# One edge tile in 44 fetched row by row from ScalarE's queue, and PSUM copies moved from ScalarE to VectorE

## The chip, the cores and the metric

The kernel runs on one core of one Trainium2 chip. The metric is the time of one execution in device microseconds (us). A core has these engines, each with its own instruction queue: TensorE (PE; its weight loads are listed as PEld), VectorE (DVE), ScalarE (ACT), GpSimd (POOL) and SyncE (SP). SP, ACT and POOL can start DMA transfers, which 16 DMA engines carry out. Engines wait for each other through semaphores.

## The reference

One layer of a relational graph network with a pre-normalization, on 12500 nodes of 256 features and 212500 edges of 8 types. Edges are sorted by destination; each node has one edge to itself as the last of its edges.

```python
h = jnp.maximum(_layernorm(x, axis=-1), 0.0)
hx = jnp.einsum('ni,rio->rno', h, weight)            # 8 relations
msg = hx[edge_type, src]
agg = jax.ops.segment_sum(msg, dst, num_segments=num_nodes)
node_repr = agg * 0.5 ** 0.5 + h_bias + (h @ loop_weight) * 0.5 ** 0.5
return x + node_repr
```

All arithmetic of the features is in float32.

## The kernel before

The order is turned round: rows of `h` are first summed by destination and type, and the sums are then multiplied by the weights.

**Edge tiles.** The edges are cut into 792 units, and each unit into two tiles (`PAIR`) of up to 128 edges, 1583 tiles in all. 128 units form a block; for each block the positions, sources and types of its edges are worked out on VectorE ahead of time (`prepare`), by small steps in a list named `background`. The sources end as a table `gidx[b]`, turned so that one column holds the 128 sources of a tile. Tile t stands in block t // 256.

**Fetching.** `gather(t)` (L779) issues one indirect DMA from POOL (L791): 128 rows of 1 KB, by the column of `gidx`, into the buffer `msg[t]`. There are buffers for 66 tiles, and the gather of tile t + 64 is issued in the turn of tile t, so it waits until PE has done with the buffer's former tiles. The first 100 tiles fetch rows of `x` and normalize them (L753); all later ones fetch rows of `h32`, the normalized table in DRAM that the kernel writes at its beginning.

**Sums by destination.** For each tile, VectorE makes one-hot rows (`onehots`, L804, four tiles at once), and PE multiplies the fetched rows with them (`edge_sums`, L837). The two tiles of a unit add up in one PSUM bank `ps`, four of which take turns. VectorE then adds the bank into a ring of sums in SBUF at an offset read from a register (`add_sums`, L851); 16 offsets at a time are loaded into VectorE's registers (L816).

**Products.** The nodes form 98 groups of 128. When a group's sums are complete, PE multiplies them with the weights of the 8 types and of the loop (L1029, 36 matmul instructions a group, spread over the following tiles by a budget), and VectorE adds the result to `x` (L1041, L1042). Six groups have their place in the ring.

**Starting a group.** `begin(g)` turns the group's rows of `h` on PE (`turn_nodes`, L878, into the PSUM bank `pt`). VectorE writes the rows, masked by the type of each node's own edge, into the ring as first values (`own`, L900, eight instructions), and ACT copies them to `self_t` (`keep`, L883), from which the loop product is made. The types come from `find_types`, once for four groups: a small product on PE (L934), some VectorE instructions (`kinds_of`), four ACT instructions that write a diagonal matrix (L954), a product that spreads it (L961) and an ACT copy `types` (L965). All these use the one bank `pt`; `shared` puts such jobs one behind the other, each with a first step and later steps some tiles afterwards.

**Order.** The whole program is unrolled, and its order written out by hand: one turn of the loop `for t in range(NT)` (L1186) per edge tile, in which every engine's queue gets its next instructions. ACT also issues 34 small transfers named `spans` (L353) for later blocks; SP issues all other plain transfers, among them three of a single row (L346).

Of the kernel before, what the change touches and what calls it, by code (L numbers as in the profile page):

```python
# [8 lines left out]

F32 = mybir.dt.float32  # L10
BF16 = mybir.dt.bfloat16
I32 = mybir.dt.int32
AF = mybir.ActivationFunctionType
ALU = mybir.AluOpType
# [2 lines left out]
DRAM = bass.MemoryType.DRAM  # L17
SYNC_DEP = mybir.DependencyInfo(mybir.DependencyClass.Sync, mybir.DependencyReason.DATA)
DVE = mybir.EngineType.DVE

P = 128
EPS = 1e-5
# [3 lines left out]
XG = 4  # L26
# [20 lines left out]

MSGS = 66
AHEAD = 64

QUAD = 4
LEAD = 4
# [167 lines left out]
def kernel(  # L220
# [32 lines left out]
    dram = ctx.enter_context(tc.tile_pool(name="dram", bufs=1, space=DRAM))  # L253

    h32 = dram.tile([N, D], F32, name="h32")

    const = ctx.enter_context(tc.tile_pool(name="const", bufs=1))
    ident = const.tile([P, P], F32, name="ident")
# [25 lines left out]
    with ExitStack() as main:  # L284
# [29 lines left out]
        msg, oh, offsets, kind = {}, {}, {}, {}  # L314
        firsts, stops, loops, marked, typed, gidx, col = {}, {}, {}, {}, {}, {}, {}
        added, zeroed = {}, {}
        state = {"h32": None}


# [52 lines left out]
        def core(got, name):  # L372

            return got[name][:, BEFORE : BEFORE + EDGES]

        def compacted(got, bit, bits, n):

# [9 lines left out]
        def sources(b, got):  # L387


            if b == 0:  # L390
                def copy():
                    nc.vector.tensor_copy(work_tile(got, "sf", 2)[:, :U], got["s"][:, :U])

                return [copy, *turned(
                    got, "sf", lambda: gidx.setdefault(b, idx.tile([P, U], I32, name="gidx")))]

            def rises():
                nc.vector.tensor_tensor(
                    work_tile(got, "rise", 0), got["d"][:, 1:], got["d"][:, :WIDE], op=ALU.subtract)

            def spans():
                got["from_"] = small.tile([P, 1], F32, name="from_")
                nc.vector.tensor_tensor(got["from_"], got["spans"][:, 0:1], steps, op=ALU.add)
                got["kept"] = small.tile([P, 1], F32, name="kept")
                nc.vector.tensor_tensor(
                    got["kept"], got["spans"][:, 0:1], got["spans"][:, 1:2], op=ALU.subtract)
                nc.vector.tensor_scalar(
                    got["kept"], got["kept"], most, limit if b == NB - 1 else float(U),
                    op0=ALU.add, op1=ALU.min)

            def stays():
                nc.vector.tensor_scalar(
                    work_tile(got, "stay", 1), got["rise"], 0.0, None, op0=ALU.is_equal)
                firsts[b] = small.tile([P, 1], F32, name="firsts")
                nc.vector.tensor_copy(firsts[b], got["d"][:, BEFORE : BEFORE + 1])

            def shifts():
                nc.vector.scalar_tensor_tensor(
                    work_tile(got, "code", 2), got["d"][:, :WIDE], got["from_"], got["stay"],
                    op0=ALU.subtract, op1=ALU.mult)  # L420

            def codes():
                nc.vector.scalar_tensor_tensor(
                    got["code"], got["code"], float(R), got["t"][:, :WIDE], op0=ALU.mult, op1=ALU.add)

            def packs():
                nc.vector.scalar_tensor_tensor(
                    packed, got["s"][:, :WIDE], float(1 << (TB + SB)), got["code"],
                    op0=ALU.mult, op1=ALU.add)

            def unpacks():
                nc.vector.tensor_single_scalar(
                    work_tile(got, "from", 5, I32)[:, :U], packed[:, :U], TB + SB,
                    op=ALU.logical_shift_right)
                nc.vector.tensor_scalar(
                    work_tile(got, "sf", 2)[:, :U], got["from"][:, :U], 0.0, float(N - 1),
                    op0=ALU.max, op1=ALU.min)
                nc.vector.tensor_single_scalar(
                    work_tile(got, "rest", 3, I32)[:, :U], packed[:, :U], (1 << (TB + SB)) - 1,
                    op=ALU.bitwise_and)  # L440

            return [rises, spans, stays, shifts, codes, packs, *compacted(got, TB, SB, WIDE), unpacks,
                    *turned(got, "sf", lambda: gidx.setdefault(b, idx.tile([P, U], I32, name="gidx")))]

        def last_edges(b, got):

# [332 lines left out]
        def gather(t):  # L779
            if t % PAIR == 0:  # L780
                both = msgs.tile([P, PAIR, D], F32, name="msg")
                for i in range(PAIR):
                    msg[t + i] = both[:, i, :]
            if t % QUAD:
                kind[t] = kind[t - 1]
            else:
                kind[t] = "h" if state["h32"] is not None and t >= state["h32"] + LATE else "x"
            table = {"h": h32, "x": x}[kind[t]]
            b, i, u = place_of(t)
            at = i * P + u  # L790
            nc.gpsimd.indirect_dma_start(  # L791
                out=msg[t], out_offset=None, in_=table[:, :],
                in_offset=bass.IndirectOffsetOnAxis(ap=gidx[b][:, at : at + 1], axis=0))

        def onehots(t):

# [25 lines left out]
        def edge_sums(t):  # L822
            m, o = msg.pop(t), oh.pop(t)
            if t % PAIR == 0:
                bank = banks[t // PAIR % BANKS]
                sums["ps"] = bank[:, : KC * R * WIN].rearrange("p (c k) -> p c k", c=KC)
            ps = sums["ps"]
            i = t % PAIR
            width = R * (REACH[0][1] if i and t // (PAIR * P) < NB - 1 else WIN)
            end = t == NT - 1 or i == PAIR - 1  # L830
            free = added.get(t // PAIR - BANKS)
            if i == 0 and free is not None and latest["pe"] is not None:
                tc.add_manual_dep(latest["pe"], free.name, SYNC_DEP, reason="bank is free")
            if i == 0 and latest["pe"] is not None:
                tc.add_manual_dep(latest["pe"], made[t], SYNC_DEP, reason="one-hots are made")
            for c in range(KC):
                j = nc.tensor.matmul(  # L837
                    ps[:, c, :width], m[:, c * P : (c + 1) * P], o[:, :width],
                    start=(i == 0 and c == 0), stop=(end and c == KC - 1))
            latest["pe"] = j.ins  # L840
            return ps

        sums = {}
# [23 lines left out]
            i = nc.scalar.activation(a, zero.unsqueeze(2).to_broadcast([P, KC * R, GROUP]), AF.Copy)  # L867
            zeroed[g, "slot"] = i.ins

        def turn_nodes(g, pool, written=None):  # L870

            n = plan.ends[g] - plan.starts[g]
            pst = pt[:, : KC * P].rearrange("p (c d) -> p c d", c=KC)

            def turn():
                rows_ = got["h", g // XG][:, g % XG, :]
                for c in range(KC):
                    nc.tensor.transpose(  # L878
                        pst[:, c, :n], rows_[:n, c * P : (c + 1) * P], ident[:n, :n])

            def keep():
                got["self", g] = pool.tile([P, KC, GROUP], F32, name="self_t")
                i = nc.scalar.activation(got["self", g][:, :, :n], pst[:, :, :n], AF.Copy)  # L883
                if written:
                    tc.add_manual_dep(
                        i.ins, written[0].name, SYNC_DEP, reason="one reader at a time")

            return turn, keep, pst

        def begin(g):  # L890

            n = plan.ends[g] - plan.starts[g]
            q, k = divmod(g, XG)
            written = []
            turn, keep, pst = turn_nodes(g, selves, written)
            s0 = g % SLOTS * GROUP

            def own(r):
# [3 lines left out]
                    op0=ALU.is_equal, op1=ALU.mult)  # L902
                if r == R - 1:
                    zeroed[g, "slot"] = i.ins
                    written.append(i.ins)

            def write():
                for r in range(R):
# [17 lines left out]
        def find_types(q):  # L926
# [11 lines left out]
            def kinds_of():  # L938
# [11 lines left out]
                nc.vector.tensor_reduce(kinds, one, AX.X, ALU.add)  # L950
                marked[q] = marks.tile(
                    [P, 2, XG * GROUP], BF16, tag="mark0", name="diagonal")[:, 0, :]
                for g in range(XG):
                    nc.scalar.activation(  # L954
                        marked[q][:, g * GROUP : (g + 1) * GROUP], ident, AF.Copy,
                        scale=kinds[:, g : g + 1])

            shared(find, [(2, kinds_of)])

# [2 lines left out]

            def types_of():
                typed[q] = types.tile([P, XG * GROUP], BF16, name="types")
                nc.scalar.activation(typed[q], pt, AF.Copy)  # L965

            shared(spread, [(1, types_of)], lambda: q in marked, wait=2 * SETTLE)

        got = {}

# [14 lines left out]
        def group_ahead(g):  # L985
# [11 lines left out]
            if q < plan.typed:  # L997
                def turned_nodes():
                    turn, keep, _ = turn_nodes(g, early)
                    shared(turn, [(1, keep)])  # L1000

                work.append((0.4, turned_nodes))
            if k == XG - 2:
# [70 lines left out]
        with tc.manual_schedule():  # L1074
# [111 lines left out]
            for t in range(NT):  # L1186
                done["tile"] = t
                if t + AHEAD < NT:
                    gather(t + AHEAD)
                blocks_ahead(t)  # L1190
                credit = min(0.0, credit) + SHARE - (0.52 if t % PAIR else 0.0)
                for f in after:
# [110 lines left out]
```

## Time and profile before

| | us |
|---|---|
| median of 3 runs (2438.91 to 2439.70) | 2439.66 |
| the profiled execution | 2440.51 |
| its span, first to last instruction | 2438.7 |
| PE busy, matmuls (10339 instructions) | 1934.7 |
| VectorE busy (3382) | 1326.8 |
| ACT busy (475) | 222.2 |
| POOL busy (1609) | 1508.5 |

The mean clock granted to TensorE is 0.893 of full speed. Busy times are of the engines' own work; instructions that only wait, branch, load registers or issue a DMA are not in them, with one exception: POOL's indirect DMAs are counted. A row of a group names the line, the engine, the operation, what it writes and reads, its count, its busy time and mean duration in ns, and the idle time of the engine before it with what ended most of that. "Issue" stands for idle time in which the engine waited for nothing that the profile shows, and "remote" for a release that the profile can't assign. The times of PE are those at which its instructions start; their ends are modelled.

### The profile page before, as it was taken

How to read it: one execution, taken by the hardware profiler on the slowest of the kernel's cores; microseconds unless marked ns; L12 is line 12 of the kernel's file. 1: busy time of each engine (PE TensorE's matmuls, PEld its weight loads, DVE VectorE, ACT ScalarE, POOL GpSimd, SP SyncE). 2: the span in 40 equal slices, each digit the busy share in tenths (PEclk: the TensorE clock that was granted, in tenths of full speed). 3: DMA queues.
4: the chain of work that ended last, by engine and by line, in shares of the span. 5: the costliest groups of instructions: out<-in, count | busy, mean ns of one | idle time of the engine just before them, and what ended most of it. 6: DMA issues, size and time to landing. Idle time of an engine off the chain costs nothing.

```text
span 2438.7 us, 28985 instructions
## 1 busy us (share of the span) xinstructions
PE 1934.7 (79%) x10339; PEld 1700.9 (70%) x10339; DVE 1326.8 (54%) x3382; ACT 222.2 (9%) x475; POOL 1508.5 (62%) x1609
## 2 busy tenths in 40 slices
PE   0257788787888888888888888888888888888889
PEld 0246677776777777777777777777777777777788
DVE  3387734546744545754445754445754445765453
ACT  3474310000000000000000000000000000000000
POOL 7535666666666666666666666666666666666640
PEclk9557989999989898998889998899899889998999
DMA  6584433343334343333343333343333343333320
GB/s 204 161 296 137 125 89 117 89 127 114 91 117 119 89 124 116 91 117 105 105 123 91 116 116 93 115 127 89 117 117 89 118 118 92 117 106 101 111 71 14
DMA packets 147869, 278.87 MB, mean 114 GB/s; under 512 B 29759, under 2 KB 97064, under 8 KB 147720
## 3 DMA queue, kind: packets, MB, share of 16 engines
q0 software_dynamic: 75984, 207.59, 29.2%
q1 hardware_dynamic: 70136, 69.38, 8.9%
q8 instruction: 82, 1.34, 0.2%
q14 instruction: 67, 0.55, 0.1%
q10 hardware_dynamic: 1600, 0.01, 0.0%
HBM read 251.26 MB, written 25.60 MB: 114 GB/s over the span
## 4 chain that ended last, share of the span: by engine, by line
PE 66%; issue 14%; DVE 11%; another core or an unknown queue 4%; ACT 2%; DMA 1%; POOL 1%; DVEq 0%; SPq 0%; ACTq 0%; POOLq 0%
PE ps L837 33%; PE po L1029 31%; DVE acc L851 2%; DVE oh L804 1%; DVE e_stats L741 1%; DVE acc L900 1%; PE pt L878 1%; DVE n_stats L741 1%; DVE moves L380 1%; DVE n_mv L743 1%; POOL msg L791 1%; DMA w<-in_L_gnn_weight_dram 1%; DVE fixed L382 0%; ACT diagonal L954 0%
## 5 line engine op out<-in xcount | busy, mean ns | idle before, releaser
L791 POOL DMA_INDIRECT msg<-h,gidx x1483 | 1411.6, 952 | 761.5 <-issue 389.6
L837 PE MATMUL ps<-oh,msg 128*128 128x176 f32 (+1 forms) x6332 | 1178.9, 314 | 303.2 <-issue 163.0
L837 PEld LDWEIGHTS ps<-oh,msg 128*128 128x128 f32 x6332 | 1090.1, 208 | 444.6 <-issue 217.5
L1029 PE MATMUL po<-w,acc 128*128 128x256 f32 x3136 | 975.0, 413 | 87.5 <-issue 75.5
L851 DVE TENSOR_TENSOR acc<-acc,ps 128x352 f32 x792 | 409.0, 516 | 764.4 <-remote 377.3
L1029 PEld LDWEIGHTS po<-w,acc 128*128 128x128 f32 x3136 | 577.8, 206 | 164.8 <-issue 132.2
L804 DVE TENSOR_TENSOR oh<-fixed,cols 128x704 f32<-128x704 f32 x397 | 348.9, 879 | 0.0
L900 DVE SCALAR_TENSOR_TENSOR acc<-types,pt 128x256 f32<-128x256 bf16 (+1 forms) x688 | 248.7, 411 | 89.2 <-PE ps L837 48.5
L883 ACT ACTIVATE self_t<-pt 128x256 f32<-128x256 f32 x98 | 37.5, 383 | 1754.2 <-DVE acc L900 1030.5
L791 POOL DMA_INDIRECT msg<-in_x_dram,gidx x100 | 95.0, 950 | 83.1 <-issue 49.3
L1029 PE MATMUL po<-wl,self_t 128*128 128x256 f32 x392 | 116.6, 410 | 14.3 <-issue 7.7
L1029 PEld LDWEIGHTS po<-wl,self_t 128*128 128x128 f32 x392 | 70.9, 201 | 35.5 <-issue 24.0
L878 PE MATMUL pt<-ident,hr 128*128 128x128 f32 x196 | 41.7, 288 | 29.0 <-issue 25.7
L1041 DVE TENSOR_TENSOR xr<-xr,po 128x256 f32<-128x256 f32 x98 | 40.6, 415 | 31.1 <-remote 14.5
L753 ACT ACTIVATE msg<-msg,e_shift,e_rstd 128x256 f32<-128x256 f32 x100 | 51.8, 589 | 21.3 <-DVE e_shift L750 12.0
L753 ACT ACTIVATE xt<-xt,n_shift,n_rstd 128x256 f32<-128x256 f32 x98 | 50.9, 589 | 18.5 <-DVE e_stats L741 6.1
L878 PEld LDWEIGHTS pt<-ident,hr 128*128 128x128 f32 x196 | 25.9, 156 | 30.2 <-issue 25.9
L954 ACT ACTIVATE diagonal<-ident,kinds 128x128 bf16<-128x128 f32 x88 | 28.1, 390 | 172.7 <-DVE kinds L950 158.6
L1042 DVE TENSOR_TENSOR xr<-xr,po 128x256 f32<-128x256 f32 x98 | 41.2, 421 | 3.4
L380 DVE TENSOR_SCALAR moves<-fixed 128x271 int32<-128x271 int32 (+1 forms) x90 | 40.5, 450 | 2.2 <-issue 0.9
L382 DVE COPY_PREDICATED fixed<-moves,fixed 128x311 int32<-128x311 int32 (+14 forms) x90 | 38.0, 422 | 3.1
L741 DVE BATCH_NORM_STATS2 e_stats<-msg 128x6 f32<-128x256 f32 x100 | 34.9, 410 | 0.0
(242 smaller groups left out, 354.8 us busy)
## 6 DMA issues: line engine op xcount, KB each, us to landing
msg<-h,gidx POOLq DMA_INDIRECT x1483
xt<-in_x_dram SPq DMA_DIRECT2D x24, 512.0 KB
h<-xt SPq DMA_DIRECT2D x24, 512.0 KB
xr<-in_x_dram SPq DMA_DIRECT2D x24, 512.0 KB
hr<-h SPq DMA_DIRECT2D x24, 512.0 KB
out_dram<-xr SPq DMA_DIRECT2D x24, 512.0 KB
w<-in_L_gnn_weight_dram SPq DMA_DIRECT2D x2, 1024.0 KB
msg<-in_x_dram,gidx POOLq DMA_INDIRECT x100
```

What stands on the lines that cost most here:

```text
L380: nc.vector.tensor_single_scalar(m, packed[:, :n], 1 << (bit + k), op=ALU.bitwise_and)
L741: nc.vector.bn_stats(stats[:n, j, :], rows_[j])
L753: nc.scalar.activation(rows_[j], rows_[j], AF.Relu, bias=shift[:n, j : j + 1], scale=rstd[:n, j : j + 1])
L791: nc.gpsimd.indirect_dma_start(out=msg[t], out_offset=None, in_=table[:, :], in_offset=bass.IndirectOffsetOnAxis(ap=gidx[b][:, at : at + 1 ...
L804: j = nc.vector.tensor_tensor(o[:, k : k + v, :i, :], iota_f.unsqueeze(1).unsqueeze(1).to_broadcast([P, v, i, C]), of.unsqueeze(3).to_broa ...
L837: j = nc.tensor.matmul(ps[:, c, :width], m[:, c * P : (c + 1) * P], o[:, :width], start=(i == 0 and c == 0), stop=(end and c == KC - 1))
L851: i = nc.vector.tensor_tensor(a, a, ps, op=ALU.add)
L878: nc.tensor.transpose(pst[:, c, :n], rows_[:n, c * P : (c + 1) * P], ident[:n, :n])
L900: i = nc.vector.scalar_tensor_tensor(acc[:, :, r, s0 : s0 + n], of, float(r + 1), pst[:, :, :n], op0=ALU.is_equal, op1=ALU.mult)
L1029: i = nc.tensor.matmul(got["out", g][:n], lhs, rhs, start=(r == R and c == 0), stop=(r == R - 1 and c == KC - 1))
L1041: nc.vector.tensor_add(rows_[:n, k, :], rows_[:n, k, :], outs[g % 2][:n, 1, :])
L1042: nc.vector.tensor_add(rows_[:n, k, :], rows_[:n, k, :], got["out", g][:n])
```

## The change

1. An odd tile t is fetched in another way if t modulo 44 is 43, it lies in a block after the first, it is fetched from `h32`, and t + 64 is below 1583. POOL issues no gather for it. Instead four steps of 32 rows are put into a list `fetches`, to be taken from eight turns later on, up to four entries per turn. The first entry of a step loads 32 byte offsets into ACT's registers (`load_sources`); it puts 32 entries in front of the list, each of which issues one DMA of one row of 1 KB from ACT's queue, at the address in the register.
2. The byte offsets are a new table `single[b]`, made by VectorE beside `gidx[b]`: the untransposed sources of the first 128 columns times 1024.
3. The landing of these rows is counted by four semaphores of their own, used in turn. PE waits for the count by an instruction of its own ahead of the tile's matmuls; the first row of a tile waits until PE has done the tile that used the counter before.
4. The copies `self_t` and `types` are made by VectorE, and the four ACT instructions for the diagonal become one of VectorE. `keep` of early groups and `types_of` come two tiles after their first step, and not one.

```diff
+SINGLE = 44
+FETCH = 4
+SOURCES = 32
+HOLD = 8
+COUNTERS = 4
...
+    h32_bytes = h32.bitcast(U8).rearrange("n d -> (n d)").unsqueeze(0)
...
+        def kept_sources(b, got):
+
+            def keep():
+                single[b] = idx.tile([P, P], I32, name="single")
+                nc.vector.tensor_single_scalar(
+                    single[b], got["sf"][:, :P], float(D * 4), op=ALU.mult)
+
+            return [keep]
...
             b, i, u = place_of(t)
+            if b and t % PAIR and kind[t] == "h" and t + AHEAD < NT:
+                if t % SINGLE == SINGLE - 1:
+                    fetched[t] = len(fetched)
+                    fetches.extend(
+                        (done["tile"] + HOLD, lambda r=r: load_sources(t, r))
+                        for r in range(0, P, SOURCES))
+                    return
             at = i * P + u
...
+        def load_sources(t, r0):
+
+            b, _, u = place_of(t)
+            _, vals = nc.values_load_multi_w_load_instructions(
+                single[b][u : u + 1, r0 : r0 + SOURCES], engines=[ACT],
+                min_val=0, max_val=(N - 1) * D * 4,
+                skip_runtime_bounds_check_because="clamped to the table where they are computed")
+            k = fetched[t]
+
+            def fetch_row(i, v):
+                j = nc.scalar.dma_start(
+                    msg[t][r0 + i : r0 + i + 1, :].bitcast(U8), h32_bytes[:, bass.ds(v, D * 4)])
+                j.then_inc(counters[k % COUNTERS], 16)
+                tc.no_tile_sem_insts.add(j.ins.name)
+                tc.add_to_no_dep_group(f"rows{t}", j.ins)
+                if i == 0 and k >= COUNTERS:
+                    tc.add_manual_dep(
+                        j.ins, summed[k - COUNTERS], SYNC_DEP, reason="counter is at rest")
+
+            for i, v in reversed(list(enumerate(vals))):
+                fetches.insert(0, (0, lambda i=i, v=v: fetch_row(i, v)))
+
+        def fetch(n):
+            for _ in range(n):
+                if fetches and fetches[0][0] <= done["tile"]:
+                    fetches.pop(0)[1]()
...
+            if t in fetched:
+                k = fetched[t]
+                j = nc.tensor.wait_ge(counters[k % COUNTERS], 16 * P * (k // COUNTERS + 1))
+                tc.declare_fence(j.ins, group=f"rows{t}")
             for c in range(KC):
...
-                i = nc.scalar.activation(got["self", g][:, :, :n], pst[:, :, :n], AF.Copy)
-                if written:
-                    tc.add_manual_dep(
-                        i.ins, written[0].name, SYNC_DEP, reason="one reader at a time")
+                nc.vector.tensor_copy(got["self", g][:, :, :n], pst[:, :, :n])
...
-                for g in range(XG):
-                    nc.scalar.activation(
-                        marked[q][:, g * GROUP : (g + 1) * GROUP], ident, AF.Copy,
-                        scale=kinds[:, g : g + 1])
+                nc.vector.tensor_tensor(
+                    marked[q].rearrange("p (g k) -> p g k", g=XG),
+                    ident.unsqueeze(1).to_broadcast([P, XG, GROUP]),
+                    kinds.unsqueeze(2).to_broadcast([P, XG, GROUP]), op=ALU.mult)
...
-                nc.scalar.activation(typed[q], pt, AF.Copy)
+                nc.vector.tensor_copy(typed[q], pt)
...
-            shared(spread, [(1, types_of)], lambda: q in marked, wait=2 * SETTLE)
+            shared(spread, [(2, types_of)], lambda: q in marked, wait=2 * SETTLE)
...
                 if t + AHEAD < NT:
                     gather(t + AHEAD)
+                fetch(FETCH)
```

More of the change, by code (lines that the diff above doesn't have):

```diff
@@ L11 @@
 BF16 = mybir.dt.bfloat16
+U8 = mybir.dt.uint8
 I32 = mybir.dt.int32
@@ L19 @@
 DVE = mybir.EngineType.DVE
+ACT = mybir.EngineType.Activation
 P = 128
@@ L316 @@
         added, zeroed = {}, {}
+        single, fetches = {}, []
+        counters = [tc.alloc_semaphore(f"rows{i}") for i in range(COUNTERS)]
+        fetched, summed = {}, {}
         state = {"h32": None}
@@ L442, in sources @@
             return [rises, spans, stays, shifts, codes, packs, *compacted(got, TB, SB, WIDE), unpacks,
-                    *turned(got, "sf", lambda: gidx.setdefault(b, idx.tile([P, U], I32, name="gidx")))]
+                    *turned(got, "sf", lambda: gidx.setdefault(b, idx.tile([P, U], I32, name="gidx"))),
+                    *kept_sources(b, got)]
         def last_edges(b, got):
@@ L840, in edge_sums @@
             latest["pe"] = j.ins
+            if t in fetched:
+                summed[fetched[t]] = j.ins.name
             return ps
@@ L868, in clear, with turn_nodes @@
             zeroed[g, "slot"] = i.ins
-        def turn_nodes(g, pool, written=None):
+        def turn_nodes(g, pool):
             n = plan.ends[g] - plan.starts[g]
@@ L893, in begin @@
             q, k = divmod(g, XG)
-            written = []
-            turn, keep, pst = turn_nodes(g, selves, written)
+            turn, keep, pst = turn_nodes(g, selves)
             s0 = g % SLOTS * GROUP
@@ L904, in own @@
                     zeroed[g, "slot"] = i.ins
-                    written.append(i.ins)
             def write():
@@ L999, in turned_nodes @@
                     turn, keep, _ = turn_nodes(g, early)
-                    shared(turn, [(1, keep)])
+                    shared(turn, [(2, keep)])
                 work.append((0.4, turned_nodes))
```

## The prediction

> **What bounds the kernel now.** I read the page first, then the groups by line, the waits, the chain in order of time, a timeline of 12 us, and windows with and without gathers.
>
> ```profile
> PE 1934.7 (79%) x10339; PEld 1700.9 (70%) x10339; DVE 1326.8 (54%) x3382; ACT 222.2 (9%) x475; POOL 1508.5 (62%) x1609
> ...
> PE 66%; issue 14%; DVE 11%; another core or an unknown queue 4%; ACT 2%; DMA 1%; POOL 1%; DVEq 0%; SPq 0%; ACTq 0%; POOLq 0%
> ...
> L791 POOL DMA_INDIRECT msg<-h,gidx x1483 | 1411.6, 952 | 761.5 <-issue 389.6
> ```
>
> TensorE (PE) is the busiest engine and carries 66% of the chain; GpSimd (POOL) carries 1%. One gather takes POOL 0.95 us and 0.30 us of issue, 1.25 us from start to start. 1583 of them are 1979 us of a 2438.7 us span, so POOL has room. The waits say who holds it:
>
> ```profile
> POOL msg L791 <- issue: 438.9, 1324, 9.9
> DVE acc L851 <- remote: 377.3, 131, 6.5
> ...
> POOL msg L791 <- remote: 219.5, 122, 2.9
> ...
> POOL msg L791 <- PE ps L837: 91.8, 79, 2.4
> ```
>
> The 438.9 us are the fixed 0.30 us per gather. The 219.5 and 91.8 us are waits for a message buffer that PE still holds. Where nothing stops it, PE is fast; this is the chain in order of time:
>
> ```profile
> 1186.67 0.60 PE ps L837 x4
> 1187.27 0.43 PE po L1029 x2
> 1187.70 0.42 PE ps L837 x4
> 1188.12 0.45 PE po L1029 x2
> ```
>
> A pair of edge tiles with four products takes 1.90 us, 0.95 us a tile, less than one gather. But it does not run like that for long (timeline, all engines, thinned):
>
> ```profile
> 1206.07 0.95 POOL L791 DMA_INDIRECT msg<-h,gidx  x1 [0.30 <-issue]
> ...
> 1207.21 0.45 PE L837 MATMUL ps<-oh,msg 128*128 128x176 f32 x1 [1.72 <-issue]
> ...
> 1208.62 0.45 PE L837 MATMUL ps<-oh,msg 128*128 128x176 f32 x1 [0.96 <-issue]
> ...
> 1209.43 0.52 DVE L851 TENSOR_TENSOR acc<-acc,ps 128x352 f32 x1 [3.86 <-remote]
> 1209.67 0.96 POOL L791 DMA_INDIRECT msg<-h,gidx  x1 [2.65 <-remote]
> ```
>
> From 1202 to 1209 us PE starts an instruction only every 0.71 us, with no wait that the profile shows ("issue"). VectorE (DVE) idles 3.9 us behind it, POOL 2.7 us. Such stops come about every 14 us, all through the gathers. I count 58 to 61 tiles (instructions of L791 against those of L837) between POOL and PE where a stop begins, 60 to 62 where it ends, so PE is never short of gathered data. They end where POOL is held by full buffers. Two windows show that they belong to the gathers:
>
> ```profile
> core 0: us, PE busy (x) PEld busy (x) DVE busy (x) ACT busy (x) POOL busy (x), PEclk, DMA share, GB/s
> 1000.00:1060.00 60.00, 50.52 (x273) 44.18 (x273) 42.37 (x120) 2.64 (x7) 40.15 (x42) 0.91 0.32 90
> 2360.00:2420.00 60.00, 60.00 (x354) 56.79 (x353) 28.02 (x52) 0.00 (x0) 0.00 (x0) 1.00 0.03 9
> ```
>
> After the last gather (2352.8 us) PE runs 60 us of 60, at full clock. In the first window its matmuls (164 of L837 at a mean of 0.13 us and 93 of L1029 at 0.216, by the chain above, and 16 others near 0.1) are 43 us of work in 60: 17 us are lost beside 42 gathers, 0.41 us each. So I read the bound as PE plus stops that gathers bring with them. What the stops are, the profile does not say.
>
> **The change part by part.** The profiled execution took 2440.5 us, 0.9 us over the median of 2439.66; 0.2% (5 us) is about what a measurement can tell from no change.
>
> *Gathers removed.* Tiles t = 43 modulo 44 that lie in a later block, hold normalized rows and have t + 64 < 1583: t = 263, 307, ... 1495, that is 29 of 1583 (1.8%). A floor: if only POOL got time, nothing, since its slack hides it. If each gather brings PE its 0.41 us, 29 x 0.41 = 12 us. If the stops end when buffers are full, a tile that POOL skips brings that one POOL interval nearer, 29 x 1.25 = 36 us; the pace itself, 139 gathers in the 200 us from 1000 us, would be 29 x 1.44 = 42 us. I take the middle of 12 and 36, 24 us, because PE must still do the 0.95 us of work of each such tile, while the stops do look tied to POOL's lead. Ends: 0 and 42.
>
> *Rows added on ScalarE (ACT).* Each such tile is 128 transfers of 1 KB and four register loads of 32 offsets. The loads: VectorE's loads of offsets (L816) take 1.10 us for 16 values and 0.60 for the last 8, so 0.062 us a value, 2.1 us for 32, 8.4 us a tile. A transfer: nothing here issues one row from a register, so two rows bound it:
>
> ```profile
> L353 ACTq DMA_DIRECT2D spans<-in_dst_dram x34: 317/434/597, 530.0 to 2038.2; - x34
> ```
> ```profile
> L346 SPq DMA_DIRECT2D nat_s<-in_src_dram x1: 296/296/296, 2037.5 to 2037.5; - x1
> ```
>
> L353 writes 16 partitions and costs 0.475 us from start to start (eight in 3.80 us at 1279.43); L346 writes one partition in one run, 0.296 and 0.04 between, 0.335 us. A tile then occupies ACT for 128 x 0.335 + 8.4 = 51 us to 128 x 0.475 + 8.4 = 69 us. If a register operation goes before each (VectorE's FUSED_REGOPS before L851, 0.069 us), it is 60 to 78 us. Due are 44 tiles x 1.44 = 63 us: the point of decision is 0.43 us a row. I take 0.335 to 0.41, 51 to 60 us, because a row is L346's form, and the offset is already multiplied to bytes on VectorE. Then rows finish some 30 us ahead of use (they start 56 tiles, 81 us, ahead) and cost the path nothing. If that cover is gone, PE waits at each such tile: the first rival. [...]
>
> Queued behind the rows on ACT: the "spans" transfers of later blocks, which VectorE needs 20 tiles (29 us) after their issue, and nothing else after the start. The rows' own wait, for PE to free a buffer of 66 tiles before, is met when they are issued. Bytes do not change; 3712 issues replace 29.
>
> *Wait added on PE.* One per such tile, behind it all later matmuls: PE's semaphore instructions take 0.051 us in the trace, 29 x 0.05 to 29 x 0.2 = 1 to 6 us; I take 2.
>
> *Copies moved from ACT to VectorE.* 98 copies of turned nodes: L365's copy of the same 128x256 from PSUM takes 0.424, so 42 us. 22 of types: 512 columns at 1.05 ns more a column (L851: 352 in 0.516, L1041: 256 in 0.415), 0.69 us, 15 us. 22 diagonals, now one instruction for four: 0.68 us by the same slope from L804 (704 in 0.883), 15 us. Six products of offsets, 2 us. Sum 74 us on an engine that is 54% busy. What hides it are VectorE's 377 and 273 us of idling before L851. Without cover it costs what its share of the chain says, 74 x 11/54 = 15 us. Against that, PE's wait for ACT's four diagonal copies (18.7 us over 8) shrinks, and the handover from VectorE to ACT and back falls away. From -5 to +15; I take 2.
>
> Sum: -24 + 0 + 2 + 2 = -20 us: 2440.5 - 20 = 2420.5 in a profiled execution, 2420 in the median.
>
> **The rivals.** *ACT is late (slower).* A row costs 0.475, as ACT's own L353 does, so a tile takes 69 us against 63. The first tile has 64 x 1.44 = 92 us, 21 us more than 69 and the 2 us of landing; after that each of 28 adds 6: 28 x 6 - 21 = 147, so about 2585. It decides from 0.43 us a row. At 0.45 it is 66 us, 28 x 3 - 24 = 60, 2500; with 0.069 on top of 0.475, some 2840. For: it is the same queue. Against: L346's form is nearer. 0.27.
>
> *Nothing comes of it.* The stops are PE's own, and POOL's slack swallows the gathers: 0 + 2 + 2 - 3, within 5 us of 2440. For: POOL carries 1% of the chain. Against: the window after the last gather. 0.14. [...]
>
> *VectorE or the rows cost more than the stops give back.* VectorE's 15 us, PE's 6, and stops that 128 small transfers bring as 1 gather did (the 0.41 us are not regained): +5 to +25, 2455. For: VectorE is saturated after each stop (3.73 us of 4 from 1180 us). 0.11.
>
> *The change does not do what it says:* if no tile met the condition, only the copies would move, 2440 to 2455; but 29 do, so this has no chance of its own.
>
> **How the numbers follow.** Forecast (faster by 6 to 48 us) 0.48; late ACT 0.27; nothing 0.14; costs 0.11. Faster 0.48, same 0.14, slower 0.38. The forecast's own range is 2392 to 2434. The range for 8 in 10 starts at 2392 (42 - 24 = 18 below the sum, and 10 for a pace that quickens) and must reach into late ACT: 2560, 0.455 us a row or so; beyond lie some 0.15 above and 0.05 below.
>
> **What would show it.** Right: 1554 gathers; ACT's issues near 0.34 to 0.41 us from start to start, with idle time between tiles; PE's waits at such tiles near nothing; fewer or shorter 0.71 us trains of PE per tile; POOL held longer by buffers. Wrong: issues of 0.45 us or more back to back and PE waiting for the rows' counter every 44 tiles (late ACT); PE's stops as frequent as before beside fewer gathers (nothing); VectorE among the releasers of PE's L837 (costs).

## The result, and the profile after

The changed kernel takes 2461.24 us in the median (2457.15 to 2462.87, four runs) against 2439.68 of the kernel before: ratio 1.0081, 95% interval 1.0068 to 1.0094. It is 0.8%, some 22 us, slower, where 20 us faster was forecast. The profiled execution took 2462.21 us (span 2460.5).

The page of the kernel after, its busy times, the chain that ended last by engine, and the group of the gathers:

```profile
PE 1928.1 (78%) x10339; PEld 1699.6 (69%) x10339; DVE 1385.1 (56%) x3530; ACT 143.6 (6%) x267; POOL 1480.6 (60%) x1580
...
PE 46%; issue 9%; DVE 5%; another core or an unknown queue 3%; POOL 1%; DMA 1%; DVEq 0%; POOLq 0%
...
L821 POOL DMA_INDIRECT msg<-h,gidx x1454 | 1383.8, 952 | 810.3 <-issue 356.1
```

The work moved as said: 29 gathers fewer, 78.6 us off ACT, VectorE busy 58 us longer, PE's matmuls no longer than before (1928.1 us against 1934.7). (The chain ends early at a wait here, so its shares are not compared.) So PE works as much in a longer span: it stops more. The waits of the kernel after (waiter, line, released by: us in total, times, longest us):

```profile
POOL msg L821 <- issue: 403.5, 1224, 7.9
DVE acc L914 <- remote: 301.7, 123, 6.0
...
PEld ps L898 <- issue: 262.2, 353, 2.2
POOL msg L821 <- remote: 235.0, 147, 2.8
PE ps L898 <- issue: 191.7, 326, 1.8
POOL msg L821 <- PE ps L898: 159.8, 123, 3.3
```

The lines of PE in the kernel before, for comparison, and its wait for VectorE in both, before first:

```profile
PEld ps L837 <- issue: 217.5, 314, 2.6
PE ps L837 <- issue: 163.0, 277, 1.8
PEld ps L837 <- DVE acc L851: 77.8, 17, 37.1
```
```profile
PEld ps L898 <- DVE acc L914: 80.7, 17, 40.6
```

POOL's work fell by 27.9 us, and its idle time under "issue" by 35.4 us. (Of these, 29 gathers at 0.30 us make 9; most of the rest belongs to gathers that now wait for a buffer instead, since the line counts 1224 gathers where it was 1324.) But its waits for buffers that PE holds rose from 219.5 + 91.8 to 235.0 + 159.8, by 83.5 us. What POOL gained it handed back waiting for PE. PE's idle time before the sums grew under "issue", where the profile names no releaser (191.7 us, 163.0 before), and hardly under VectorE.

Was ACT late? The row's line, the register loads and PE's new wait, from the views of one line (duration in ns, least/median/most; first and last start in us):

```profile
L835 ACTq MOVE msg<-h x3712: 2/29/782, 348.3 to 2301.0; - x196
L835 ACTq DMA_DIRECT2D msg<-h x3712: 2/228/876, 427.1 to 2301.2; - x196
```
```profile
L828 ACTq TENSOR_LOAD <-single x116: 1120/2260/3202, 345.8 to 2286.9; - x116
```
```profile
L895 PEldq EVENT_SEMAPHORE  x29: 51/51/51, 515.0 to 2337.8; - x29
```

No. A row takes 0.318 us from start to start (median in the records of L835), a tile's rows 55 to 60 us from first to last in 18 of 29 tiles (53.5 to 64.5 in all) where 63 are due, and PE's 29 waits take 0.051 us each: the rows have always landed. (The last row starts at 2301.2 us, and PE takes up its tile at 2337.8.) Yet tile 255 starts at 507.2 us (before: 507.4) and tile 1500 at 2343.5 (2322.2; starts of PE's matmuls in the trace): all of the loss builds up while rows are issued. Two windows, one beside rows and gathers, one after the last gather (2374.2 us):

```profile
core 0: us, PE busy (x) PEld busy (x) DVE busy (x) ACT busy (x) POOL busy (x), PEclk, DMA share, GB/s
1000.00:1060.00 60.00, 49.47 (x272) 44.20 (x271) 45.33 (x129) 0.00 (x0) 38.08 (x40) 0.91 0.32 91
2380.00:2440.00 60.00, 60.00 (x356) 56.83 (x355) 28.71 (x53) 0.00 (x0) 0.00 (x0) 1.00 0.03 9
```

It is the picture of before: stops beside the gathers, none after them. One of the stops, in the timeline of the kernel after:

```profile
1013.66 9.05 ACTq L835 DMA_DIRECT2D msg<-h  x9
...
1017.95 0.38 PE L1087 MATMUL po<-w,acc 128*128 128x256 f32 x1 [1.09 <-issue]
...
1020.05 0.38 PE L1087 MATMUL po<-w,acc 128*128 128x256 f32 x1 [1.72 <-issue]
...
1022.44 0.94 POOL L821 DMA_INDIRECT msg<-h,gidx  x1 [2.45 <-remote]
```

PE is in its slow step, and so is ACT: nine rows in 9.05 us where they take 0.318 each. The trace shows no wait of ACT there. This stop is not PE's alone.

### The profile page after: what moved, and what is told of

Its sections match the earlier page's. It is cut to its first block, busy times and chain, and to the rows that moved or that the text cites. A ratio compares the mean times of both kernels' runs of the same rounds, so it can differ in the third digit from the quotient of the medians.

```text
span 2460.5 us, 36283 instructions
## 1 busy us (share of the span) xinstructions
PE 1928.1 (78%) x10339; PEld 1699.6 (69%) x10339; DVE 1385.1 (56%) x3530; ACT 143.6 (6%) x267; POOL 1480.6 (60%) x1580
## 3 DMA queue, kind: packets, MB, share of 16 engines
q10 hardware_dynamic: 9024, 3.82, 0.7%
## 4 chain that ended last, share of the span: by engine, by line
PE 46%; issue 9%; DVE 5%; another core or an unknown queue 3%; POOL 1%; DMA 1%; DVEq 0%; POOLq 0%
PE ps L898 23%; PE po L1087 22%; DVE acc L914 1%; POOL msg L821 1%; DVE acc L959 1%; PE pt L941 1%; DVE oh L861 1%; DMA msg<-h,gidx 1%; DVE moves L402 0%; DVEq L873 0%; DVE fixed L404 0%; PE pt L1019 0%; DVE diagonal L1011 0%; DVE self_t L946 0%
## 5 line engine op out<-in xcount | busy, mean ns | idle before, releaser
L821 POOL DMA_INDIRECT msg<-h,gidx x1454 | 1383.8, 952 | 810.3 <-issue 356.1
L898 PE MATMUL ps<-oh,msg 128*128 128x176 f32 (+1 forms) x6332 | 1182.0, 314 | 335.1 <-issue 191.7
L1087 PE MATMUL po<-w,acc 128*128 128x256 f32 x3136 | 961.6, 408 | 88.3 <-issue 78.4
L914 DVE TENSOR_TENSOR acc<-acc,ps 128x352 f32 x792 | 408.6, 516 | 662.1 <-remote 301.7
L1087 PEld LDWEIGHTS po<-w,acc 128*128 128x128 f32 x3136 | 571.7, 203 | 170.4 <-issue 132.8
L946 DVE COPY self_t<-pt 128x256 f32<-128x256 f32 x98 | 40.7, 415 | 6.7 <-PE po L1087 3.2
L1019 PE MATMUL pt<-diagonal,ones_b 128*128 128x512 bf16 x22 | 10.5, 476 | 32.1 <-DVE diagonal L1011 23.2
```

The source lines that it names most:

```text
L821: nc.gpsimd.indirect_dma_start(out=msg[t], out_offset=None, in_=table[:, :], in_offset=bass.IndirectOffsetOnAxis(ap=gidx[b][:, at : at + 1 ...
L898: j = nc.tensor.matmul(ps[:, c, :width], m[:, c * P : (c + 1) * P], o[:, :width], start=(i == 0 and c == 0), stop=(end and c == KC - 1))
L914: i = nc.vector.tensor_tensor(a, a, ps, op=ALU.add)
L946: nc.vector.tensor_copy(got["self", g][:, :, :n], pst[:, :, :n])
L1087: i = nc.tensor.matmul(got["out", g][:n], lhs, rhs, start=(r == R and c == 0), stop=(r == R - 1 and c == KC - 1))
```

## The experiments

The experiments stand in five sets. Each set ran on a chip of its own, with runs of the kernel before beside it, and these differ (2462.6, 2441.7, 2440.2, 2465.5 and 2027.2 us). So only ratios to before are compared between sets, and microseconds are a ratio times the set's own time of before. The code excerpts show the main lines only; where fewer transfers are issued, the count that PE waits for is lowered to match.

**Which part costs?** Four kernels: the copies alone; the rows alone; the gathers dropped with nothing in their place; the whole change with its 29 gathers kept.

```diff
 e1_copies  -                if t % SINGLE == SINGLE - 1:
            +                if False:
 e2_rows    (the copies of turned nodes, types and diagonals back on nc.scalar)
 e3_skip    (before)
            +            if b and t % 44 == 43 and kind[t] == "h" and t + AHEAD < NT:
            +                msg[t] = msg[t - 1]
            +                return
 e4_both                 for r in range(0, P, SOURCES))
            -                    return
```

> The kernel before with only the copies moved: turned nodes, types and diagonals are written by VectorE, every tile is gathered by GpSimd, ScalarE fetches no row. 'The copies cost' (VectorE carries 58 us more work, and a stop of PE lasts until VectorE has caught up): +10 to +22 us, so 2450 to 2461, most of the 21.6 us of the whole change. 'The rows cost' (128 single-row transfers bring PE stops as gathers did): within 5 us of 2440. The term of my prediction for this part was +2, ends -5 and +15.

Measured: 2460.61 against 2462.64, 0.9988 (0.9979 to 0.9996): 3 us faster. VectorE's extra 58 us cost nothing. By itself this part of the change is a gain, though hardly more than can be told.

> The kernel before with the 29 gathers dropped and nothing in their place: each such tile multiplies the rows of the tile before it, so its own rows are left out of the sums. It prices a dropped gather alone. My prediction's term (24 us, ends 12 to 42): 2398 to 2428. 'POOL's slack swallows them, the stops are PE's own': within 5 us of 2440. If it is near 2440, the term of -24 is what failed, and the rows or copies add the 21.6 us; if it is near 2416, the rows and copies together cost some 46 us.

Measured: 2425.46, 0.9848 (0.9834 to 0.9861): 37 us faster, 1.29 us for each dropped gather. The stops do hang on the gathers, at the price of one POOL interval (29 x 1.25 = 36).

> The whole change, but the 29 gathers stay as well: each such tile is gathered by GpSimd and then fetched again row by row into the same buffer. Against the whole change it prices the 29 gathers beside the rows. If a dropped gather gives PE 0.41 to 1.44 us: +12 to +42 us over 2461. If dropped gathers give nothing: 2456 to 2466. ScalarE's rows now wait for the gather of their tile, 64 tiles ahead, which has landed before they start 8 tiles later, so no new wait is expected.

Measured: 2523.78, 1.0238 (1.0224 to 1.0252). Over the copies alone it is 0.0250 or 62 us, 2.1 us for each tile fetched by rows, 16.6 ns a row. Against the whole change (1.0081) it is 39 us, 1.33 us for each of the 29 gathers, which agrees with e3. The parts add up: -37 - 3 + 62 = +22.

> The whole change without the moved copies: 29 tiles are fetched row by row by ScalarE, 29 gathers are gone, the copies stay on ScalarE, between the rows. 'The rows cost': +15 to +25 us, 2455 to 2465. 'The copies cost': 0 to -24 us, 2416 to 2440, as my prediction's -24 for the gathers says. One thing may disturb it: a copy on ScalarE now waits its turn behind queued rows, a step of 0.32 us each, and PE's L1019-like products wait for it.

Measured: 2538.97, 1.0285 (1.0255 to 1.0316): 50 us worse than the whole change, by another cause, which its chain and its waits name:

```profile
PE 35%; ACTq 30%; issue 19%; DVE 9%; another core or an unknown queue 4%; ACT 2%; DMA 1%; POOL 0%; DVEq 0%; SPq 0%; POOLq 0%
```
```profile
ACT self_t L946 <- issue: 785.2, 34, 36.4
```

The copies stand behind rows and register loads in ACT's order, up to 36.4 us, and PE's jobs in the bank `pt` wait for them (its L997 72.4 us over 9 times). The disturbance that the expectation named was the larger part, so this run does not price the rows; e4 does. It does show what moving the copies to VectorE was good for: without it the change would have cost 70 us.

**What in a row costs?** All four have the copies moved and the gathers kept, as e4. The loads alone (without PE's wait); the transfers from fixed addresses, without loads and moves; the 128 rows in one transfer; a quarter of the rows.

```diff
 f1_loads    -            for i, v in reversed(list(enumerate(vals))):
             -                fetches.insert(0, (0, lambda i=i, v=v: fetch_row(i, v)))
 f2_fixed    -            _, vals = nc.values_load_multi_w_load_instructions(...)
             +            vals = [(r0 + i) * D * 4 for i in range(SOURCES)]
 f3_one      +                    msg[t], h32[:P, :])
 f4_quarter  -                        for r in range(0, P, SOURCES))
             +                        for r in range(0, SOURCES, SOURCES))
```

> As e4_both (copies moved, all gathers kept), but of the rows only the 116 register loads of 32 offsets are left on ScalarE: no row is transferred and TensorE waits for none. e4_both stood 63 us over e1_copies; the question is which part of a row carries it. 'The loads' (TENSOR_LOAD, 2.14 us each, 248 us in all): +63 over the copies alone, a ratio to before near 1.024. 'The transfers': as the copies alone, a ratio of 0.999.

> As e4_both, but the 3712 rows come from fixed addresses (the first 128 rows of the table): no register loads and no register moves, the same transfers of 1 KB, counters and wait of TensorE. The 29 tiles therefore sum other rows. 'The transfers and their semaphores carry it': a ratio to before near 1.024, as e4_both. 'Each instruction on ScalarE carries it' (two per row before, now one): about half, 1.011. 'The loads carry it': 0.999. TensorE's wait for the counter costs nothing by e2's and the change's trace (0.05 us) and stays in.

> As f2_fixed, but all 128 rows of a tile in one transfer of 128 KB: 29 issues in place of 3712, the same bytes into the same buffers, the same wait of TensorE. 'The number of issues carries it': as the copies alone, a ratio of 0.999 to 1.002. 'The bytes, the wait or the counters carry it': 1.02.

> As e4_both, but only the first 32 of a tile's 128 rows are fetched by ScalarE (over the gathered ones), one register load a tile in place of four. If each row costs the same, 63/4 = 16 us over the copies alone: a ratio of 1.005. If what costs is per tile (the wait, the counter): 1.02. If what costs is that ScalarE issues nearly without a pause (55 of 63 us, now 14), so that TensorE is left no rest: under 1.003.

Measured: f1 0.9986 (0.9976 to 0.9995), f2 1.0202 (1.0185 to 1.0219), f3 0.9985 (0.9976 to 0.9995), f4 1.0050 (1.0033 to 1.0067). f1 does not price the loads: its trace holds none of the 116 on ACT, only the 116 semaphore instructions of that line (in the kernel after there are 116 loads). So f1 is the copies alone once more, and the base of this set. Against it the same bytes in 29 transfers cost nothing; 3712 transfers cost 53 us over f3 (0.0217 x 2441.65), 14.3 ns each, with no load or register move among them; a quarter of the rows costs 15.6 us over f1, a quarter of e4's 62. The added time lies in PE's slow steps: after 430 us, gaps of 0.6 to 2.2 us between the starts of its matmuls add up to 372 us in f1, 378 in f3, 405 in f4 and 444 in f2 (trace records; a rough measure, which sets e1 and e3 only 7 us apart where their times differ by 35). The price goes by the row, not by the tile, and neither TensorE's wait nor the counters have a part in it: f3 has both. The remaining 9 us of e4 over f2 (0.0036, about the size of the two intervals together) may belong to the loads, the register moves or the changing addresses; no run separates them.

**The issue or the completion?** f3's transfer of 128 rows left 16 packets beside those of its rows (its queue q10 has 5776 packets: 1600 that the kernel before has too, 3712 of rows and 29 x 16), where a transfer of one row left one (q10 of the kernel after: 3712 packets of 1 KB, and 5312 of four bytes, 3712 more than before; trace records). I took these packets for reports that a transfer has ended; the trace gives their size, not their purpose. If a transfer of 16 rows leaves 16 as well, 8 of them a tile have the packets of 128 single rows and a sixteenth of the issues. In the same set: the whole change with one transfer in place of 128; register moves alone; and half of all gathers dropped.

```diff
 h1_sixteen   +                    msg[t][r0 : r0 + 16, :], h32[r0 : r0 + 16, :])
 h2_skip_one  (f3_one)
              +                    return
 h3_moves     (f3_one) +                for _ in range(2):
              +                    nc.scalar.reg_mov(spare, 1)
 e5_half      (before) +            if b and t % 2 and kind[t] == "h" and t + AHEAD < NT:
              +                msg[t] = msg[t - 1]
              +                return
```

> As f2_fixed (copies moved, all gathers kept, rows of fixed addresses, which are other rows), but a tile's 128 rows go in 8 transfers of 16 rows: 232 issues in place of 3712, and, as f3's transfer of 128 rows left 16 four-byte semaphore packets, 16 of them from each, so 3712 semaphore packets as in f2 and the same 3712 packets of 1 KB. 'The issues carry the cost' (53 us over 3712, 14 ns each): 232 of them 3 us, a ratio to before of 0.999 to 1.001. 'The completion writes carry it' (53 us over 3248 more of them, 16 ns each): 1.020.

Measured: 2439.44, 0.9996 (0.9987 to 1.0006): 3 us over f3, within the two intervals, and as 232 issues at 14 ns make it (3.3), not 53. The queue's packets are the same, first f2_fixed's page, then h1_sixteen's, and its DMA view's count of issues:

```profile
q10 hardware_dynamic: 9024, 3.82, 0.7%
```
```profile
q10 hardware_dynamic: 9024, 3.82, 0.6%
...
msg<-h ACTq DMA_DIRECT2D x232, 16.0 KB
```

9024 packets in both (1600 + 3712 + 3712, and 1600 + 3712 + 232 x 16): what costs here goes with the number of transfers started (53 us for 3712; 3 us, within the two intervals, for 232), not with the bytes or the number of packets. The trace does not say on which DMA engines a packet ran, so a different spread of single rows over them is not excluded.

> The whole change, but a tile's 128 rows come in one transfer of 128 KB from fixed addresses (other rows than the tile's own): 29 gathers gone, copies moved, wait of TensorE and counters as they are. If the parts add up as measured so far (dropped gathers -37, copies and one transfer -4): -40 us, a ratio of 0.984. If a gather's cost only comes back because its tile must be moved by somebody: near 0.999.

Measured: 2399.96, 0.9836 (0.9821 to 0.9851): 40 us faster, as added up. The whole distance from here to the change, 0.0245 or 60 us, is that its rows come one by one.

> As f3_one, and 256 register moves on ScalarE after each such tile's one transfer, 7424 in all, which transfer nothing. 'Every instruction that ScalarE issues costs TensorE time' (e4 over f2: 9 us for 3712 moves and 116 loads; 61 us for 7424 instructions, 8 ns each): a ratio of 1.02. 'Only those that start a transfer do': 0.999; at the 2.4 ns a move that e4 over f2 would allow, 18 us, 1.006.

Measured: 0.9992 (0.9982 to 1.0001). Inconclusive: the trace holds none of the 7424 moves, though it records 3712 such moves in the kernel after, and the queue that the page calls "instruction" (q14) has 65 packets, as in f3 (the kernel after has 124). So the kernel that ran was f3 again, and says only that f3's ratio comes out again within its interval.

> The kernel before with every second gather dropped, some 630 in all, each such tile multiplying the rows of the tile before it. It tells whether the stops of TensorE belong to the gathers. 'They do': with POOL free half the time they go nearly all, TensorE is left with 0.95 us a tile, and some 450 to 600 us are saved, 1840 to 1990. 'They are TensorE's own': the stops stay, and 0 to 100 us are saved. A straight line through e3_skip (1.28 us each) would be -810, below TensorE's own work, so it must bend.

Measured: 1901.11, 0.7791 (0.7777 to 0.7805): 539 us faster for 631 gathers fewer (POOL x978 for x1609), 0.85 us each, less than e3's 1.29 because PE's own work ends it. Its window:

```profile
1000.00:1060.00 60.00, 60.00 (x383) 56.57 (x382) 42.79 (x93) 3.34 (x9) 28.08 (x30) 1.00 0.34 101
```

In this window PE stands at 60 of 60 at full clock, with 30 gathers beside it. Stops came beside 42 gathers in such a window (before), not beside 30.

**Any queue? And by itself?** For i1 the rows of f2 move to SyncE; i2 and i3 have half the gathers, with and without f2's rows.

```diff
 i1_sp          -                j = nc.scalar.dma_start(
                +                j = nc.sync.dma_start(
 i2_half_fixed  (f2_fixed)
                +                if t not in fetched:
                +                    msg[t] = msg[t - 1]
                +                return
 i3_half        (the same, and if False: for the rows)
```

> As f2_fixed (copies moved, all gathers kept, 3712 rows of fixed addresses, other rows than the tile's), but the rows are issued by SyncE's queue in place of ScalarE's. 'Any issuing queue costs it': a ratio to before near 1.020, as f2_fixed. 'It is ScalarE's place that matters': 0.999. SyncE's stores of finished rows stand in the same order as the rows; if TensorE then waited for the counter, the trace would show waits of TensorE for the rows, and the time above 1.020 would be theirs.

Measured: 2502.24, 1.0156 (1.0139 to 1.0173): 41 us over the copies alone, 11 ns an issue. Most of the price goes along to the other queue. PE's 29 waits for the rows still take 0.051 us each, so it is no lateness of SyncE.

> As f2_fixed, with every second gather dropped as in e5_half (such a tile multiplies the rows of the tile before it, or, one in 22, the fixed rows): the 3712 issues where TensorE has hardly a stop. 'An issue costs TensorE 14 ns by itself': 53 us over i3_half. 'It costs only through the stops beside dense gathers': within 8 us of i3_half, since TensorE stood at 60 us of 60 with 30 gathers beside it.

> As i2_half_fixed without the fixed rows: copies moved, every second gather dropped, nothing in its place. It is the base for i2_half_fixed; by e5_half and the copies' -3 us it should come to 0.775 to 0.781 of before.

Measured: i2 1922.52, 0.7795 (0.7779 to 0.7811), i3 1920.56, 0.7794 (0.7781 to 0.7807): 3712 issues for 0.0001, between -5 and +5 us. PE's gaps of 0.6 to 2.2 us after 430 us are 24 us in i2 and 27 in i3. Their windows, i2 first:

```profile
1000.00:1060.00 60.00, 60.00 (x382) 56.57 (x381) 41.92 (x91) 0.00 (x0) 27.63 (x30) 1.00 0.34 102
```
```profile
1000.00:1060.00 60.00, 60.00 (x382) 56.55 (x382) 42.38 (x94) 0.00 (x0) 27.84 (x30) 1.00 0.32 99
```

So 3712 issues cost PE nothing by themselves that these runs can tell. They cost 53 us (f2) where gathers are dense enough to bring stops.

**What do the stops follow?** Half the buffers and half the lead; one and two memsets of 8 columns behind each gather.

```diff
 j1_ahead   -MSGS = 66
            -AHEAD = 64
            +MSGS = 34
            +AHEAD = 32
 j2_pause   +            for _ in range(1):
            +                nc.gpsimd.memset(pause, 0.0)
 j3_pause2  (the same with range(2))
```

> The kernel before with the copies moved (e1_copies, ratio 0.999) and half the message buffers: 34 in place of 66, gathers 32 tiles ahead in place of 64. 'The stops end where GpSimd is held by full buffers': they come as often, at a lead of 26 to 31 tiles where it was 58 to 63, and the time stays within 0.5%. 'The depth of the lead brings them': fewer stops and a time under 0.98.

> e1_copies with one memset of 8 columns on GpSimd behind each gather (its memsets take 0.10 us), so that it issues a gather every 1.36 us or later where it was 1.25, still under the 1.44 us a tile of the whole. 'What is short is a rate of about one gather in 1.44 us, however they are spaced': the time stays (0.997 to 1.005) and GpSimd is held less by buffers. 'Dense bursts bring the stops': most of the 485 us of stops go, and the time falls towards 1.36 us a tile, 100 us less, a ratio of 0.96.

> As j2_pause with two memsets behind each gather, 1.47 us or more from gather to gather. By the rate: GpSimd becomes the bound and the time rises to about 1.47 us a tile, a ratio of 1.02 to 1.03, with few stops left. By the bursts: the same ratio near 1.02, but then j2 stands well below both.

Measured: 1.0150 (1.0133 to 1.0167), 1.0118 (1.0101 to 1.0135), 1.2870 (1.2848 to 1.2891). But on this set's chip the kernel before itself took 2027.2 us, 17% less than on all others, and the premise did not hold. j2's window of 60 us shows the difference:

```profile
1000.00:1060.00 60.00, 56.57 (x336) 48.45 (x336) 41.23 (x94) 0.00 (x0) 51.48 (x95) 1.00 0.36 104
```

POOL issues a gather every 1.26 us and is hardly held (28.1 us of its waits are for PE's sums; the memset of 0.127 us fits into the 0.30 us that it had between gathers), and PE is short of data: 291.5 us of its weight loads' waits are for messages, over 426 waits. Gaps of 0.68 to 0.75 us between the starts of PE's matmuls and weight loads, 299 in e1_copies, are 23 in j1 and some 25 in j2. So on this chip the same program hardly stops at this density, POOL is the bound, and the three runs tell nothing on their question. They do show that one gather in 1.44 us is no limit on this chip: here it is one in 1.26. What the change would do there was not run.

## Why the prediction was wrong

**The step that failed is "rows added on ScalarE: 0".** Its working held: the row's step was bounded at 0.335 to 0.475 us and taken at 0.335 to 0.41, measured 0.318; a load of 32 at 2.1 us, measured 2.16 in the mean; a tile at 51 to 60 us, measured mostly 55 to 60 against 63 due (that match is in part luck: 128 steps of 0.318 and four loads make 49 us, and the rest is time in which ACT itself was held); rows ahead of use, and PE's wait is 1.5 us in all. The conclusion "cost the path nothing" did not follow. I asked whether ACT would be on time, and priced the transfers by ACT's time alone. They cost PE 62 us (e4 over e1), through the stops that I had already seen and had put down to gathers, without asking what else brings them.

**Gathers removed: -24 taken, -37 measured** (34 to 41 by e3's interval), inside the ends 0 and 42. The mechanism with the end of 36, a stop that ends one POOL interval sooner, gives the size, but no run shows that mechanism by itself: j1 was to test where stops end, on the chip that hardly has any. Averaging it with 0.41 us a gather, which is the mean loss and not what one gather more or less changes, took a third of it away.

**Copies: +2 taken, -3 measured**; the 15 us without cover did not come, and VectorE's longer work stayed under its idling before L914 (301.7 us of "remote", 377.3 before). The moved instructions themselves took 72 us where 74 were taken (98 x 0.416, 22 x 0.691, 22 x 0.683 and six of 0.22 us); VectorE's busy time grew by only 58. **PE's wait: 2 taken, 1.5 measured**, 29 at 0.051 us; no trace shows the 0.2 us of its upper end.

**The rivals.** Late ACT, 0.27, is out: PE waits nowhere for rows (0.051 us at each of the 29 tiles). The trace has 0.228 us for the transfer and 0.029 for the move, 0.318 from start to start, well below the 0.43 us a row from which that rival decides. "Nothing comes of it", 0.14, is out by e3. The third, 0.11, has the sign and nearly the time (2455, measured 2461), but half of that is luck: of its three prices VectorE's 15 came out as -3 and PE's 6 as 1.5, while "stops that 128 small transfers bring as 1 gather did" is the cause, at 2.1 us a tile and not one gather's 0.41. And it let the gathers give nothing, where they gave 37. That 2461 lies inside the wide range, 2392 to 2560, is luck too: its upper end was there for late ACT, which did not come.

So the move was no exchange of equals: on the chips where PE stops, 128 issues on ACT cost PE 2.1 us (e4) where the one gather that they replace had cost 1.29 (e3).

**What stays open** is what a stop is. Shown: it comes beside dense gathers (e3, e5); issues of single transfers on ACT or SP lengthen the time lost to it, by 11 to 17 ns each (f2, f4, i1), and do nothing where gathers are sparse (i2 against i3); and on one chip of those that ran it is nearly absent (j1, j2). That issuing engines share something is my guess, which would fit most of that, though in a stop POOL (1.25 us from gather to gather), and ACT in f2, keep their own step; no run shows it.

## What to carry to other kernels

Price a transfer that is moved to an idle engine's queue by the number of issues as well as by that engine's time: here 3712 transfers that were always on time cost the busiest engine 53 to 62 us, the same bytes in 29 or 232 transfers 0 to 3. Where an engine stands still and the profile names no releaser, ask what else in the program could bring the same stop, and look in the trace whether other engines slow down in the same microseconds, before booking a gain. And before copies are left on an engine that takes on a long queue of transfers, look who waits for them: moving them here was worth some 50 us.

## What the runs showed of the hardware that was not expected

- A stop took hold of an engine besides PE that was issuing just then. Between instructions without a wait, ACT was idle for 0.60 to 0.75 us 245 times in the kernel after and never in the kernel before, where it issues far less (after 430 us); with the rows on SyncE (i1) it was SyncE, 300 times. PE's step in a stop is the same 0.70 us, and both keep the same beat: in the stop shown above, ACT starts an instruction at 1017.22, 1019.32, 1020.02 and 1020.72 us, PE at 1017.25, 1019.35, 1020.05 and 1020.74 (trace records). That beat is common to engines for which the trace shows no wait on each other. POOL does not take it up: in the same stop its gathers start every 1.25 us until 1019.05 us, and then it waits for a buffer.
- With rows from fixed addresses (f2) ACT hardly shows that step (4 times) though PE loses 53 us: who is held need not be who brings it.
- The kernel before took 2438 to 2469 us on the chips of four sets and 2022 to 2029 us on that of the fifth, where the stops were nearly gone.
- Two memsets behind each gather (j3) brought the mean step between gathers far above their own time: 0.28 us of memsets, but 2608.5 us in all. The timeline shows gathers alternately 1.37 and 1.86 us apart, the longer with 0.62 us of "issue". Why was not looked into.
